# A graph-attention layer's softmax step and its feed-forward parts: one row copied by another engine, one more part a chunk in the last block

## The chip, the cores and the metric

The kernel runs on one core of a Trainium2 chip. The metric is the device time in microseconds (us) of one launch. The engines are TensorE (PE, matrix products; PEld is its weight load), VectorE (DVE), ScalarE (ACT), GpSimd (POOL, which issues the indirect gathers and scatters) and SyncE (SP, which issues the plain transfers). Each works off its own queue in order, and they meet through semaphores.

## The reference, cut to what matters

There are two graph layers in a row over 1250 nodes with 512 features and 40000 edges; only the first is touched.

```
h = layer_norm(x, ln1_g, ln1_b)                         # first layer
xl, xr = (h @ Wl), (h @ Wr)                             # 8 heads of 64
e  = einsum(leaky_relu(xl[src] + xr[dst], 0.2), att)    # a score per edge and head
m  = segment_max(e, dst);  ex = exp(e - m[dst])
h  = segment_sum(ex / denom[dst] * xl[src]) + gat_bias  # softmax over a node's edges
x1 = x + h
x1 = x1 + gelu(layer_norm(x1) @ W1 + b1) @ W2 + b2      # feed-forward, 512 -> 2048 -> 512
x  = layer_norm(x + x1)
...                                                     # second layer: relu(x[src] + edge features), sums, two dense layers
```

## The kernel before, in words

**Tiling.** The nodes are sorted by their number of edges and laid out in ten blocks of 128, one node a partition. `KB` (L699) gives the edge slots of each block: 44, 40, 37, 35, 33, 32, 31, 29, 27, 25. The blocks go in `ORDER` (L714) from block 9 down to block 0, so block 0, with the most edges, is the last one of the first layer. A block's slots are cut into groups (L1677 to L1680) of at most 20; block 0 has groups of 20, 16 and 8, block 1 of 16, 16 and 8, the others have two. There are 22 groups. A group is cut into chunks of at most `CN` = 5 slots; 77 chunks in all. The three groups of block 0 have 4, 4 and 2 chunks.

**A chunk.** `scores` (L1540) has POOL gather one row of `xl_t` per slot into a tile `xg` (seven buffers, `GB`), forms the score with four DVE instructions and writes it to the group's tile `S`, one row of eight heads per slot. After a group's last chunk `softmax` (L1559) finds the running maximum `m`, puts the older maximum into the row behind the group's scores, and subtracts; `exp` (L1572) makes the weights `w` of the scores and of that last row, which is the factor by which the sums so far must shrink. `weigh` (L1588), which runs one group behind the scores, multiplies the rows of `xg` by `w` (some rows on ACT, the rest on DVE) and adds them up on PE in `sums`; `leave` (L1615) folds the two sums into `pacc`, and `merge` (L1627) adds that to the block's `acc`. A buffer of `xg` is free for the next gather when PE has added it up.

**A finished block.** `head_of` (L1388) makes the residual sum, the layer norm and its transpose `hT`. `body_of` (L1441) is the feed-forward: 16 slices of 128 hidden features, in steps that the code calls parts. A part is four products into `pu`, a Gelu on ACT from `pu` to `uT` (one part later), and a product of `uT` (three parts later) into `py`. There is one `py` buffer, so only one block's feed-forward runs at a time. `end_of` (L1467) makes the last norm `xo`, adds the bias to give `order` (a reused tile) and scatters it into `xb_t`. The second layer, `second` (L1774), gathers from `xb_t` and can begin only when all ten blocks are there.

**The order of the work.** Every engine's queue is written out by the Python loops: `inorder` (L775) ties each instruction of DVE, ACT, PE and POOL behind the one recorded before. The main loop (L1686 to L1739) goes over groups and chunks. In each chunk it records the scores, steps the blocks that are between attention and end (`step_others`, L1504; in block 0 once more ahead of the scores, L1703), and spends a `quota` (L1726) of feed-forward parts with `some` (L1528), which calls `part` (L1519); `part` does nothing where no block is ready. The quota is 4 where a block waits for its feed-forward (`ready`), else 3. After the last group, what is left is recorded without a quota (L1740 to L1752).

Of the kernel before, what the change touches and what calls it, by code (L numbers as in the profile page):

```python
# [11 lines left out]
OP = mybir.AluOpType  # L12
AX = mybir.AxisListType
# [700 lines left out]
ORDER = range(NB - 1, -1, -1)  # L714
# [11 lines left out]
def gnn_kernel(ctx, tc, x, src, dst, edge_attr, ln1_g, ln1_b, Wl, Wr, att, gat_bias,  # L726
# [48 lines left out]
    def inorder(engine):  # L775

        latest = {}

        class Kept:
            def __getattr__(self, name):  # L780
                def call(*args, **kw):
                    ins = getattr(engine, name)(*args, **kw)  # L782
                    if latest:
                        tc.add_manual_dep(ins.ins, latest["ins"].ins.name, no_sync, reason="order of the program")
                    latest["ins"] = ins
                    return ins
                return call
        return Kept()
# [25 lines left out]
    with ExitStack() as s0:  # L814
# [18 lines left out]
        V, A, T = (inorder(e) for e in (nc.vector, nc.scalar, nc.tensor))  # L833
# [412 lines left out]
    def attention(s1, xb_t, xo_t, eb_t, back, lone, follow):  # L1246
# [8 lines left out]
        V, A, T, G = (inorder(e) for e in (nc.vector, nc.scalar, nc.tensor, nc.gpsimd))  # L1255
# [34 lines left out]
        def normed_of(b):  # L1290
            blk = dict(b=b, xn=bp.tile([P, D], F32, name="xn"))
            get(blk["xn"], hn_t, v_c[:, b:b + 1])
            return blk

        def slots_of(b):

            s_n = ap.tile([P, KB[0]], I32, name="s_n")
            s_f = ap.tile([P, KB[0]], F32, name="s_f")
            get(s_n[:, 0:KB[b]], src_v, w_i[:, b:b + 1])
            for _ in range(3):  # L1300
                yield
            to_src(V, s_f[:, 0:KB[b]], s_n[:, 0:KB[b]], b)
# [8 lines left out]
        def rows_of(blk):  # L1311
            held["xx"] += 1
            blk["xx"] = bp.tile([P, D], F32, name="xx", bufs=3)
            get(blk["xx"], x, v_c[:, blk["b"]:blk["b"] + 1])
# [31 lines left out]
        def wr_order():  # L1346

            w_t = w1[:, 0, :].rearrange("p (k d) -> p k d", k=KD)
            yield "late"
            pts = []  # L1350
            for k in range(KD):
                pts.append(aq.tile([P, KD, P], F32, name="pt1", tag="pu", bufs=4))
                for r in range(KD):
                    T.transpose(pts[k][:, r, :], wr[:, r, k * P:(k + 1) * P], ident)
            yield
            for k in range(KD):
                A.copy(w_t[:, k, :], pts[k].rearrange("p r n -> p (r n)"))
            yield "late"
            pms = []
            for r in range(KD):  # L1360
                pms.append(aq.tile([P, KD, P], F32, name="pm", tag="pu", bufs=4))
                for k in range(KD):
                    T.matmul(pms[r][:, k, :], w_t[:, k, r * P:(r + 1) * P], order[:, k, :], start=True, stop=True)
            yield
            for r in range(KD):
                A.copy(wr[:, r, :], pms[r].rearrange("p k n -> p (k n)"))

        done, ready, going, others, pres, lates = [], [], [], [], [], []
# [128 lines left out]
        def step_pres():  # L1497

            todo = list(pres)
            pres.clear()  # L1500
            for t in todo:
                step(t)

        def step_others():  # L1504

            if done and not held["head"]:
                held["head"] = 1
                others.append(head_of(done.pop(0)))
            for t in list(others):
                step(t)  # L1510
# [15 lines left out]
        quota = [0]  # L1526

        def some(n):  # L1528
            for _ in range(min(n, quota[0])):
                quota[0] -= 1  # L1530
                part()

        def drain(what, most):
            while held[what] > most:
                step_pres()
                step_others()
                part()
                step_lates()

        def scores(g, c):  # L1540

            c0, cn = g["cuts"][c]
            xg = gp.tile([P, CN, XW], F32, name="xg")
            for j in range(cn):
                at = KO[g["b"]] + g["k0"] + c0 + j
                get(xg[:, j, :], xl_t, src_i[:, at:at + 1])
            z = ap.tile([P, CN, XW], F32, name="z")
            z4, x4 = (t.rearrange("p n (h c) -> p n h c", c=CX)[:, :cn] for t in (z, xg))
            nxr = g["blk"]["nxr"]
            for op, c_, d_ in ((OP.max, 0, RIGHT + 1), (OP.min, RIGHT + 1, CX)):  # L1550
                V.tensor_tensor(z4[:, :, :, c_:d_], x4[:, :, :, c_:d_],
                                nxr[:, None, :, c_:d_].to_broadcast([P, cn, HEADS, d_ - c_]), op=op)
            zm = z4[:, :, :, LEFT + 1:RIGHT + 1]
            V.tensor_tensor(zm, zm, sgn[:, None, :, :].to_broadcast([P, cn, HEADS, MID]), op=OP.mult)
            V.tensor_reduce(g["S"][:, c0:c0 + cn, :].rearrange("p n h -> p (n h)"),
                            z[:, :cn, :].rearrange("p n (h c) -> p (n h) c", c=CX), axis=AX.X, op=OP.add)
            g["xg"].append(xg)

        def softmax(g):  # L1559

            n, S, blk = g["n"], g["S"], g["blk"]
            m_old = blk["m"]
            m = sp.tile([P, HEADS], F32, name="m")
            V.tensor_reduce(m, S[:, :n, :].rearrange("p n h -> p h n"), axis=AX.X, op=OP.max)
            V.tensor_tensor(m, m, m_old, op=OP.max)
            V.tensor_copy(S[:, n, :], m_old)
            blk["m"] = m
            g["w"] = w = sp.tile([P, GN + 1, HEADS], F32, name="w")
            V.tensor_tensor(S[:, :n + 1, :], S[:, :n + 1, :], m[:, None, :].to_broadcast([P, n + 1, HEADS]),
                            op=OP.subtract)  # L1570
# [112 lines left out]
        blk = dict(b=ORDER[0], nxr=nxr9)  # L1683
        ahead = weighing = None
        piece = [0]
        for i, g in enumerate(groups):  # L1686
            if g["first"]:
                if i:
                    blk, ahead = ahead, None
                blk["m"] = low  # L1690
                if g["b"] == 0:
                    drain("acc", 2)
                    held["acc"] += 1
                    blk.update(over)
                    blk["acc"] = bp.tile([P, D], F32, name="acc", bufs=3)
                    nc.sync.dma_start(blk["acc"], oa_t)
            g["blk"] = blk
            g["S"] = sp.tile([P, GN + 1, HEADS], F32, name="S", bufs=2)
            nc_ = len(g["cuts"])
            left = len(groups[i - 1]["cuts"]) if i else 0  # L1700
            for c in range(nc_):
                step_pres()
                if g["b"] == ORDER[-1]:  # L1703
                    step_others()
                scores(g, c)
                if c == nc_ - 1:
                    softmax(g)
                if c == 0:
                    if not i:
                        others.append(wr_order())  # L1710
                    if g["first"] and g["b"] != ORDER[-1]:
                        others.append(slots_of(g["b"] - 1))
                    if g is groups[-1] and held["xx"] < 3:
                        rows_of(blk)
                    weighing = weigh(groups[i - 1]) if i else None
                if folded:
                    merge(folded.pop())
                if c == 1 and g["first"] and g["b"] != ORDER[-1]:
                    ahead = normed_of(g["b"] - 1)
                if c == 2 and g["first"] and ahead:  # L1720
                    others.append(xr_of(ahead))
                if i > 3 and piece[0] < len(pieces):
                    piece_of(piece[0])
                    piece[0] += 1
                step_others()
                quota[0] = 4 if ready else 3  # L1726
                todo = -(-left // (nc_ - c))
                left -= todo
                for _ in range(todo):
                    next(weighing)  # L1730
                if left == 0 and weighing:
                    next(weighing, 0)
                if not todo:
                    for _ in leave():
                        some(1)
                if c == nc_ - 1:
                    exp(g)
                some(quota[0])
                step_lates()  # L1739
# [281 lines left out]
```

## Time and profile before

| | us |
|---|---|
| median of three runs | 1482.53 (1481.47 to 1487.09) |
| the profiled execution's own time | 1477.38 |
| its span, first to last instruction | 1475.5 |
| first gather of the attention | 85.7 |
| block 0's first softmax / last scores end | 772.8 / 830.7 |
| last block's attention ends (acc) | 851.7 |
| last scatter into `xb_t` / first gather from it | 899.6 / 903.6 |
| last gather of the second layer | 1329.5 |

Busy shares of the span: PE 79%, DVE 78%, POOL 59%, ACT 48%. The mean granted TensorE clock is 0.917 of full speed. In a profile line of the timeline, the first number is the start in us, the second the duration in us, then the engine, the source line (L782 stands for all calls through the recording helper), the operation, out<-in by tile names with partitions and elements, how many instructions are merged (PE counts each fp32 product as two), and in brackets the idle time before it and what ended it. A line of waits has the waiting instruction, the one it waited for, the total in us, the number of waits and the longest. A line of windows has the length, each engine's busy us with its instructions, the granted clock (PEclk), the share of the DMA queues and GB/s. In the page's strips a digit is the busy share of a fortieth of the span, in tenths.

### The profile page before, as it was taken

The page shows a single profiled execution, that of the slowest core. Times are in us where ns is not written, and L with a number is a line of the kernel's source. Part 1 is how long each engine was busy: PE and PEld are TensorE (multiplying, and loading weights), DVE is VectorE, ACT ScalarE, POOL GpSimd, SP SyncE. Part 2 cuts the span into 40 slices and gives each one's busy share as a digit, 9 for nine tenths or more (in the row PEclk, how much of TensorE's full clock was granted, in tenths as well). Part 3 has the DMA queues.
Part 4 walks back from the last instruction along what each step waited for, and adds up shares of the span by engine and source line. Part 5 has one row for each costly group of instructions (what it writes and reads, how often), then busy time and mean ns, then how long its engine had stood idle before and what let it go on. Part 6 is the DMA issues. An engine that isn't in the chain of part 4 may idle for free. (4 is left out here: it accounts for less than half of the span.)

```text
span 1475.5 us, 16467 instructions
## 1 busy us (share of the span) xinstructions
PE 1168.7 (79%) x5204; PEld 557.0 (38%) x5204; DVE 1146.9 (78%) x1472; ACT 710.4 (48%) x2033; POOL 864.8 (59%) x789
## 2 busy tenths in 40 slices
PE   6845659898988886969787896778786998988893
PEld 4431114344544442424244363222222443335452
DVE  7859898978888889797799713988888789877133
ACT  4526366867777675776858641111111222221533
POOL 2367877755677777774754004777777777750002
PEclk9977779999999798989898998999999999999996
DMA  6246966655566756653644144778777788750001
GB/s 235 90 139 184 393 189 175 181 147 152 153 192 176 207 167 191 173 155 110 172 121 112 32 156 145 243 237 247 242 242 231 233 246 249 235 161 22 0 0 72
DMA packets 89151, 251.16 MB, mean 170 GB/s; under 512 B 17214, under 2 KB 19268, under 8 KB 88543
## 3 DMA queue, kind: packets, MB, share of 16 engines
q0 software_dynamic: 61008, 199.11, 46.5%
q1 hardware_dynamic: 28047, 50.91, 9.7%
q8 instruction: 43, 0.70, 0.2%
q14 instruction: 53, 0.43, 0.1%
HBM read 225.86 MB, written 24.22 MB: 169 GB/s over the span
## 5 line engine op out<-in xcount | busy, mean ns | idle before, releaser
L782 POOL DMA_INDIRECT xg<-xl_t,src_i x333 | 421.2, 1265 | 192.6 <-issue 113.5
L749 POOL DMA_INDIRECT xs<-xb_t,src_i x333 | 314.8, 945 | 115.0 <-issue 67.9
L782 ACT ACTIVATE xg<-xg,w 128x64 f32<-128x64 f32 x1296 | 323.2, 344 | 0.1
L782 PE MATMUL sums<-xg,ident 64*64 64x512 f32 x1332 | 208.1, 699 | 110.0 <-DVE xg L782 103.2
L1829 PE MATMUL pe<-we,eaT 64*128 64x512 f32 x666 | 201.5, 663 | 72.4 <-DVE xs L1874 67.9
L782 DVE TENSOR_TENSOR z<-xg,nxr 128x1440 f32<-128x1440 f32 (+4 forms) x154 | 197.7, 1324 | 41.0 <-DMA xg<-xl_t,src_i 40.0
L782 DVE TENSOR_REDUCE S<-z 128x32 f32<-128x2080 f32 (+2 forms) x77 | 192.2, 2496 | 2.6
L782 PEld LDWEIGHTS pu<-hT,w 128*128 128x128 f32 x1280 | 165.1, 198 | 67.5 <-issue 57.6
L1874 DVE TENSOR_TENSOR xs<-xs,pe 128x1024 f32<-128x1024 f32 (+1 forms) x130 | 153.3, 1186 | 36.8 <-DMA xs<-xb_t,src_i 24.5
L782 PE MATMUL py<-w,uT 128*128 128x512 f32 x320 | 164.7, 606 | 15.5 <-ACT uT L782 15.4
L782 PE MATMUL pu<-hT,w 128*128 128x128 f32 x1280 | 173.6, 284 | 0.0
L1875 DVE SCALAR_TENSOR_TENSOR pd<-xs,pd 128x1024 f32<-128x1024 f32 (+1 forms) x130 | 155.7, 1197 | 3.3
L782 PEld LDWEIGHTS sums<-xg,ident 64*64 64x64 f32 x1332 | 58.1, 152 | 249.8 <-DVE xg L782 127.6
L1829 PEld LDWEIGHTS pe<-we,eaT 64*128 64x128 f32 x666 | 58.3, 192 | 169.5 <-DVE xs L1874 119.1
L1871 ACT ACTIVATE xs<-pe 128x1024 f32<-128x1024 f32 x40 | 41.0, 1024 | 163.9 <-PE pe L1870 126.3
L782 DVE TENSOR_TENSOR xg<-xg,w 128x1024 f32<-128x1024 f32 (+2 forms) x77 | 102.2, 1332 | 0.0
L782 ACT ACT_TABLE_LOAD x73 | 93.7, 1283 | 7.9 <-DVE sh L782 4.3
L1870 PE MATMUL pe<-xs,ident 128*128 128x512 f32 x160 | 88.3, 662 | 3.9 <-DMA xs<-xb_t,src_i 3.7
L741 POOL DMA_INDIRECT out_dram<-z,v_i x10 | 10.0, 1003 | 130.9 <-ACT z L782 128.4
L782 PE MATMUL pacc<-ab,fold 128*64 128x512 f32 x88 | 54.3, 703 | 40.1 <-ACT ab L782 38.8
L782 DVE TENSOR_TENSOR z<-z,sgn 128x768 f32<-128x768 f32 (+2 forms) x77 | 78.2, 1016 | 0.0
L782 PE MATMUL pz<-z,v 128*128 128x512 f32 (+1 forms) x192 | 71.1, 530 | 6.0 <-ACT z L782 6.0
(264 smaller groups left out, 1286.5 us busy)
## 6 DMA issues: line engine op xcount, KB each, us to landing
eb_t<-fe SPq DMA_DIRECT2D x38, 256.0 KB
ea<-eb_t SPq DMA_DIRECT2D x38, 256.0 KB
w<-in_L_gnn_W_dram SPq DMA_DIRECT2D x8, 1024.0 KB
xg<-xl_t,src_i POOLq DMA_INDIRECT x333, 3.9
xs<-xb_t,src_i POOLq DMA_INDIRECT x333, 3.8
v<-in_L_gnn_W_dram SPq DMA_DIRECT2D x2, 2048.0 KB
xo_t<-xo SPq DMA_DIRECT2D x10, 256.0 KB
x_out<-xo_t SPq DMA_DIRECT2D x10, 256.0 KB
```

What stands on the lines that cost most here:

```text
L741: s = nc.gpsimd.indirect_dma_start(out=table, out_offset=bass.IndirectOffsetOnAxis(ap=idx, axis=0), in_=rows, in_offset=None, bounds_check ...
L749: return nc.gpsimd.indirect_dma_start(out=rows, out_offset=None, in_=table, in_offset=bass.IndirectOffsetOnAxis(ap=idx, axis=0))
L782: ins = getattr(engine, name)(*args, **kw)
L1829: nc.tensor.matmul(pe[:, k, :], eaTs[n][r, j // 2, :], we[r, :], start=True, stop=not by_pe(i))
L1870: nc.tensor.matmul(pe[:, k, :], ident, xs[:, k, :], start=False, stop=True)
L1871: nc.scalar.activation(xv, pe, AF.Relu)
L1874: add = nc.vector.tensor_add(xv, xv, pe[:, :m, :])
L1875: nc.vector.scalar_tensor_tensor(pv, xv, 0.0, pv, op0=OP.max, op1=OP.add)
```

## The change

The softmax no longer forms the new maximum in two steps. ACT copies the older maximum into the row behind the group's scores when the group's tile is made, ahead of its first chunk; the reduction then takes that row along, and a combining step and a copy on DVE are left out. Separately, the quota is 4 in all chunks of block 0, not only in those in which a block is ready.

```diff
         def softmax(g):
 
             n, S, blk = g["n"], g["S"], g["blk"]
-            m_old = blk["m"]
             m = sp.tile([P, HEADS], F32, name="m")
-            V.tensor_reduce(m, S[:, :n, :].rearrange("p n h -> p h n"), axis=AX.X, op=OP.max)
-            V.tensor_tensor(m, m, m_old, op=OP.max)
-            V.tensor_copy(S[:, n, :], m_old)
+            V.tensor_reduce(m, S[:, :n + 1, :].rearrange("p n h -> p h n"), axis=AX.X, op=OP.max)
             blk["m"] = m
...
             g["blk"] = blk
             g["S"] = sp.tile([P, GN + 1, HEADS], F32, name="S", bufs=2)
+            A.copy(g["S"][:, g["n"], :], blk["m"])
             nc_ = len(g["cuts"])
...
                 step_others()
-                quota[0] = 4 if ready else 3
+                quota[0] = 4 if ready or g["b"] == ORDER[-1] else 3
                 todo = -(-left // (nc_ - c))
```

In the queues that come out, DVE has 44 instructions fewer and ACT 22 copies more. In block 0 six of the feed-forward parts of block 1 stand ahead of the last group's `w` that stood behind it before, ACT loads its function tables four times fewer, the end of block 2 (`xo`, `order` and, on POOL, its scatter into `xb_t`, ten instructions earlier) comes two chunks sooner, and one small load of `ea` on SP changes places with its neighbour. The other instructions stand in the order they had.

## The prediction

> **What bounds the kernel now.** I read the page's slices, then the waits, then the timeline by engine around the two edits. VectorE (DVE) is at 8 or 9 tenths through the first layer, TensorE (PE) close behind, so a DVE saving can count there and a PE addition can hurt.
>
> ```profile
> PE   6845659898988886969787896778786998988893
> DVE  7859898978888889797799713988888789877133
> DVE z L782 <- DMA xg<-xl_t,src_i: 40.0, 16, 5.9
> POOL xb_t L782 <- DVE order L782: 83.6, 3, 53.2
> ```
>
> The third line (waits) says that DVE is not the bound throughout: in 16 places it waits for gathered rows. The fourth is the turn to the second layer: GpSimd (POOL) cannot gather from xb_t before block 0, the last, is through its feed-forward.
>
> A group's softmax, from DVE's timeline:
>
> ```profile
> 808.40 0.38 DVE L782 TENSOR_REDUCE m<-S 128x8 f32<-128x128 f32 x1
> 808.82 0.17 DVE L782 TENSOR_TENSOR m<-m 128x8 f32<-128x8 f32 x1
> 808.90 0.17 DVE L782 COPY S<-m 128x8 f32<-128x8 f32 x1
> 809.10 0.30 DVE L782 TENSOR_TENSOR S<-S,m 128x136 f32<-128x136 f32 x1
> ```
>
> And block 0's end:
>
> ```profile
> 815.38 0.69 DVE L782 TENSOR_TENSOR order<-xo,be_b 128x512 f32<-128x512 f32 x1 [4.58 <-ACT xo L782]
> 833.84 0.26 ACT L782 ACTIVATE w<-S 128x72 f32<-128x72 f32 x1
> 836.52 0.26 DVE L782 TENSOR_REDUCE gd<-w 128x8 f32<-128x64 f32 x1
> 850.99 0.69 DVE L782 TENSOR_TENSOR acc<-acc,t 128x512 f32<-128x512 f32 x1
> 865.32 0.69 DVE L782 TENSOR_TENSOR xx<-xx,py 128x512 f32<-128x512 f32 x1 [7.54 <-PE py L782]
> 866.05 1.12 PE L782 MATMUL py<-b,one 1*128 1x512 f32 x2 [0.78 <-DVE xx L782]
> 869.64 0.37 ACT L782 ACTIVATE uT<-pu,cols 128x128 f32<-128x128 f32 x1
> ```
>
> The last group's weights (w) come 2.7 us before DVE wants them (836.52). Attention ends at 851.68; block 0's feed-forward starts only at 866.05, when block 1's has left py; its first Gelu is at 869.64.
>
> **Edit 1: the softmax.** Of 0.70 us from m<-S to S<-S,m (808.40 to 809.10), 0.42 is the reduction's own step (to 808.82). Eight more elements add 0.01 (383 ns for 128 inputs, 396 for 136). So a group saves 0.70 - 0.43, about 0.26; 22 groups, 5.8 us of DVE. ScalarE (ACT) pays 22 copies; nearest row, COPY oden<-pd 128x8 at 172 ns: 3.8 us, on an engine 48% busy. [...]
>
> The reduction now waits for ACT. The order of the changed kernel has the copy right behind the previous group's w<-S, which ran at most about 5 us after its scores (809.10 to 814.33), while the next reduction comes 18 us later or more (709.49 to 727.56). So it costs nothing; if ACT were later, the reduction, this group's exp and the next multiply would stand behind it, and with them the buffers that POOL waits for.
>
> How much of 0.26 a group arrives, by DVE's waits. Groups 1 to 3 end before it waits for rows at 159.09: lost. Groups 4 to 9 (188.6 to 358.9) see no such wait: 6 x 0.26 = 1.6. Groups 10 to 13 (398 to 509) lie where POOL issues almost back to back (383 to 531) and DVE waits for rows six times: lost. Groups 14 to 17: half, 0.5. Groups 18 and 19: 0.5. Sum 2.6 (bounds 0 and 5.0 for the 19 groups). Against it the ACT copies where ACT is the late one: bounds 0 and 19 x 0.17 = 3.2; I take 0.5, as most of ACT's time has gaps. Up to block 0: -2.1.
>
> **Edit 2: four parts a chunk in block 0.** No work is added; the order decides. Of block 1's 16 Gelus, 9 stood before the last group's w<-S and 7 behind; now 15 and 1. ACT has four table loads fewer. [...] here a load starts at 868.35 and the Gelu behind it at 869.64, so 1.29, 5.2 in all. [...]
>
> *The tail gains.* From acc (851.68) to block 0's hT nothing stands between any more: transposes 0.97 with their wait, aT 1.14, px 1.10, sum 0.72, statistics 0.94, root 0.33, two small ones 0.5, h 0.85, transposes 0.7, hT 1.51: 8.8 us. Then xo of block 1, one table load and the first Gelu, about 11.5 after acc. Before it was 18.0 (851.68 to 869.64). Gain 6.5.
>
> *The block loses.* (a) Block 2's body ends sooner, so its xo and order<-xo move from the start of the last group to two chunks before. There DVE stands in front of order<-xo; ACT's xo stands behind hT of block 1, that behind PE's transposes of h, those behind the sums of the chunk that DVE has just multiplied (about 795.3). Sums 2.79, transposes 0.66, hT 1.5, xo 0.8: DVE waits 5.8 instead of 4.58. Moreover PE has had nothing since the sums of the chunk before (about 787), 8 us, and after a shorter rest it ran at half clock:
>
> ```profile
> 801.27 5.38 PE L782 MATMUL sums<-xg,ident 64*64 64x512 f32 x20 [3.81 <-DVE xg L782]
> core 0: us, PE busy (x) PEld busy (x) DVE busy (x) ACT busy (x) POOL busy (x), PEclk, DMA share, GB/s
> 801.00:807.00 6.00, 5.73 (x21) 1.98 (x22) 5.90 (x8) 5.97 (x22) 3.61 (x3) 0.52 0.57 164
> ```
>
> The same sums took 2.79 at clock 1.00. So another 0 to 2.6; I take 2.3. (b) From there on PE is the chain, since a part holds it 1.75 us (Gelus at 874.54, 876.30). Without the half clock: order at 801.1, order 0.7, scores of four rows 5.5, multiply 1.75: the third chunk's sums start at 809.1 and take 2.7; four parts 7.0; sums 2.7; four parts 7.0; 828.5. The two pacc steps 2.75 (820.50 to 822.25, and 1.0), two chunks' sums 3.7: 835.0. Three parts to the last Gelu that w<-S stands behind, 2 x 1.75 + 1.05 + 0.3 = 4.9; eight row products 1.9, table load 1.3, w 0.3: 843.4. DVE wanted w at 836.5: late by 6.9, and by 9.2 with the half clock. The rest of the attention follows it step by step.
>
> Sum of edit 2, with block 0's three softmaxes in it: +9.2 - 6.5 = +2.7; bounds +0.4 (full clock) and, if the cover were ample, -6.5.
>
> POOL: the scatter to xb_t of block 2 moves ahead of ten instructions, so four gathers and an xx gather and four more stand behind it. It waits for order, about 804; the first four rows then land by about 813 and are wanted at 818, the last four (free once the third chunk's sums are done, 814) at 827. Free. SP swaps one small ea load: free.
>
> **Total.** -2.1 + 2.7 = +0.6. The profiled execution took 1477.38 (span 1475.5), so 1478.0 for its like. It lies 5 us under the median 1482.53, below all three timed runs; the sum is a difference, so I put it on the median: 1483.1, say 1483.
>
> **Rivals.**
> 1. *The extra parts fit under DVE.* DVE has one wait in 750 to 838, and PE is busy 74 of those 88 us, 14 free for 10.5 us of six parts. Against: the sums and the Gelus stand in one order, so gaps before sums are not free for parts behind them. Then the tail's 6.5 stays, and -2.1 and 0.8 for three softmaxes: -9.4, 1473. Chance 0.12.
> 2. *PE stays cold (slower).* Place: block 0 from 795 to 843. With more waits inside it, PE falls to half clock again and again; the chain of eleven parts and four sums, about 34 us, stretches. Before, 800 to 838 was granted 0.91. It decides from about 0.75: 34 x (0.91/0.75 - 1) = 7.3 us more, +8, 1491. Chance 0.14.
> 3. *Edit 1 arrives whole,* the block at full clock: -5.0 + 0.4, 1478. Chance 0.16.
> 4. *Edit 1 is lost to waits for rows and to ACT:* 0.5 + 2.7, 1486. Chance 0.16.
>
> **Numbers.** The likeliest, 1483, has 0.42, with about 3 us either side. About 0.5% (7.4 us) is what a measurement can tell from no change. Faster by more: rival 1's, 0.12. Slower by more: rival 2's and an edge of rival 4, 0.15. Within: 0.73. The range goes from 1476 to 1489: it holds the likeliest, 3 and 4, and leaves most of 1 and 2 out.
>
> **What would show it.** Step 1: S<-S,m 0.44 us behind m<-S, no wait for ACT in m<-S. Step 2: order<-xo waits 6 to 8 us two chunks earlier; a wait of 6 us or more of gd for w in the last group; attention's last acc 6 to 9 us later, counted from block 0's start; the first Gelu of block 0 about 11.5 us behind acc instead of 18. Wrong if gd doesn't wait (rival 1), if the clock in that stretch is under 0.8 (rival 2), or if m<-S waits for ACT.

## The result, and the profile after

The changed kernel takes 1486.92 us (median of 15 runs, 1482.27 to 1491.26), the kernel before, timed beside it, 1482.28 (15 runs, 1477.43 to 1487.09): ratio 1.004, 95% interval 1.003 to 1.0051, so 4.4 to 7.6 us slower. The forecast was 1483, within 0.5% of before. The measured difference reaches to the edge of that 0.5%, on the slow side.

The profiled execution of after took 1488.24 us (span 1486.5), 11.0 us more than that of before. Cut at four events, the two spans differ like this:

| stretch | before | after | difference |
|---|---|---|---|
| start to block 0's acc<-px,xx | 784.41 | 784.89 | +0.48 |
| "the block": from there to the end of the last acc<-acc,t | 67.27 | 80.16 | +12.89 |
| "the tail": from there to the second layer's first gather | 51.89 | 45.73 | -6.16 |
| second layer to the end | 571.9 | 575.7 | +3.8 |

The last line is no effect of the change: the four kernels e1 to e4 below, with one part of the change or both, have 572.4 to 572.9 there. What is left, +7.2, goes with the measured 4.4 to 7.6.

DVE's timeline of after, the softmax of a group of block 0, its end and the last group. The columns are start, duration, engine, line, operation, tiles and shapes, and in brackets the idle time before it with the releaser:

```profile
804.03 0.69 DVE L782 TENSOR_TENSOR order<-xo,be_b 128x512 f32<-128x512 f32 x1 [8.24 <-ACT xo L782]
...
817.48 0.40 DVE L782 TENSOR_REDUCE m<-S 128x8 f32<-128x136 f32 x1
817.91 0.30 DVE L782 TENSOR_TENSOR S<-S,m 128x136 f32<-128x136 f32 x1
...
849.80 0.27 DVE L782 TENSOR_REDUCE gd<-w 128x8 f32<-128x64 f32 x1 [8.10 <-ACT w L782]
...
864.36 0.69 DVE L782 TENSOR_TENSOR acc<-acc,t 128x512 f32<-128x512 f32 x1
```

The softmax is two steps, 0.43 us apart, and m<-S waits for nobody (in all 22 groups together 0.5 us). The sum order<-xo stands two chunks earlier and waits 8.24 us. The last group's gd waits 8.10 us for w; before it waited not at all.

PE's timeline of after in the same stretch:

```profile
795.85 5.32 PE L782 MATMUL sums<-xg,ident 64*64 64x512 f32 x20 [7.98 <-DVE xg L782]
...
802.74 3.84 PE L782 MATMUL pu<-hT,w 128*128 128x128 f32 x32
809.55 1.12 PE L782 MATMUL py<-w,uT 128*128 128x512 f32 x2 [2.97 <-ACT uT L782]
811.97 5.38 PE L782 MATMUL sums<-xg,ident 64*64 64x512 f32 x20 [1.30 <-DVE xg L782]
817.29 1.50 PE L782 MATMUL pu<-hT,w 128*128 128x128 f32 x8
...
824.84 2.79 PE L782 MATMUL sums<-xg,ident 64*64 64x512 f32 x20
...
836.57 1.07 PE L782 MATMUL pacc<-ab,fold 128*64 128x512 f32 x2 [0.73 <-ACT ab L782]
...
848.37 1.95 PE L782 MATMUL sums<-xg,ident 64*64 64x512 f32 x16
```

The same 20 sums take 2.79 us at full clock (at 824.84, granted 1.00), and twice here 5.3 to 5.4, at about half of it (granted 0.52 and 0.50): once behind a rest of 7.98 us and once behind two short rests of 2.97 and 1.30. From 811.97 to 850.32 PE has one gap, of 0.73 us. So in the stretch that ends with the last w it is PE that sets the time.

The view of windows, for the block alone, before and then after (columns: length, then busy time of PE, PE's weight loads, DVE, ACT and POOL, the granted clock, DMA share, GB/s):

```profile
784.41:851.68 67.27, 54.46 (x312) 23.87 (x310) 54.41 (x68) 48.38 (x148) 17.62 (x14) 0.95 0.26 75
```

```profile
784.89:865.05 80.16, 63.24 (x350) 29.63 (x350) 53.91 (x64) 47.94 (x153) 19.55 (x14) 0.89 0.21 62
```

PE is busy 8.8 us longer (a net 38 matmul records more, for the parts drawn forward, and one more stretch at half clock) and idle 4.1 us longer (16.9 instead of 12.8): together the 12.9. DVE and ACT do the same work as before.

### The profile page after: what moved, and what is told of

The parts are those of the page before. It is cut to its first block, busy times and chain, and to the rows that moved or that the text cites. A ratio compares the mean times of both kernels' runs of the same rounds, so it can differ in the third digit from the quotient of the medians.

```text
span 1486.5 us, 16450 instructions
## 1 busy us (share of the span) xinstructions
PE 1174.3 (79%) x5204; PEld 559.2 (38%) x5204; DVE 1141.4 (77%) x1428; ACT 708.3 (48%) x2051; POOL 873.8 (59%) x789
## 5 line engine op out<-in xcount | busy, mean ns | idle before, releaser
L782 POOL DMA_INDIRECT xg<-xl_t,src_i x333 | 429.7, 1290 | 185.3 <-issue 102.3
L1827 PE MATMUL pe<-we,eaT 64*128 64x512 f32 x666 | 204.8, 674 | 72.6 <-DVE xs L1872 68.0
L782 ACT ACTIVATE uT<-pu,cols 128x128 f32<-128x128 f32 x160 | 55.5, 365 | 46.8 <-PE pu L782 46.0
```

Of the source, the lines that this page charges most:

```text
L1827: nc.tensor.matmul(pe[:, k, :], eaTs[n][r, j // 2, :], we[r, :], start=True, stop=not by_pe(i))
```

## The experiments

Theory 1: the time is lost where DVE stands in front of order<-xo. Theory 2: PE's chain loses it; the six parts now stand in front of the last sums on PE, whatever DVE does. Rival: the softmax loses it (22 ACT copies, or rows that come late).

The first four runs were timed on a chip on which the kernel before takes 1481 us, as above; the later ones on two others, on which it takes 1598 and 1609 us. Ratios are always to the kernel before on the same chip. From the profiles of the other chips only the block and the tail are compared, in which equal instructions last equally long (20 sums at full clock 2.79 us, z<-xg,nxr of five slots 2.93 to 2.94 on all three). Each row has one profile. How much that can differ show e1 and f3, whose instructions in the block are the same: 67.74 and 70.37. So differences of up to some 2.6 us in one block are not told from chance.

| run | ratio, 95% interval | block | tail | both |
|---|---|---|---|---|
| before | 1 | 67.27 | 51.89 | 119.16 |
| after | 1.004, 1.003 to 1.0051 | 80.16 | 45.73 | 125.89 |
| e1 softmax only | 1.0011, 0.9993 to 1.0028 | 67.74 | 51.90 | 119.64 |
| e2 parts only | 1.0041, 1.0028 to 1.0054 | 79.82 | 45.71 | 125.53 |
| e3 order later | 1.002, 1.0007 to 1.0033 | 76.97 | 47.31 | 124.28 |
| e4 last exp first | 1.0042, 1.0024 to 1.0059 | 80.15 | 45.73 | 125.88 |
| f1 order and scatter later | 1.0037, 1.0018 to 1.0056 | 77.03 | 47.20 | 124.23 |
| f2 extra matmuls | 1.0102, 1.0052 to 1.0152 | 82.30 | 45.71 | 128.01 |
| f3 weights later | 1.0066, 1.0041 to 1.0091 | 70.37 | 51.88 | 122.25 |
| f4 softmax, order later | 1.0012, 0.9992 to 1.0031 | 67.80 | 51.88 | 119.68 |
| g1 matmuls in the gap | 1.0059, 1.0038 to 1.008 | 79.79 | 45.69 | 125.48 |
| g3 early transposes | 0.999, 0.9964 to 1.0017 | 68.64 | 48.83 | 117.47 |
| g4 the same, order later | 1.0013, 0.9984 to 1.0041 | 68.56 | 48.85 | 117.41 |
| g5 early transposes, quota 3 | 0.9958, 0.9936 to 0.998 | 67.17 | 49.49 | 116.66 |

### Which part costs: e1 and e2

e1 is the kernel before with the softmax and the ACT copy alone; e2 is it with one line alone:

```diff
-                quota[0] = 4 if ready else 3
+                quota[0] = 4 if ready or g["b"] == ORDER[-1] else 3
```

> The kernel before with the softmax part of the change alone (ACT's copy of the older maximum behind the scores, one reduction over n+1 rows); quota stays 3. My theory (the softmax helps a little, the four parts cost the time): ratio to before 0.997 to 1.000, about 1480, with S<-S,m 0.38 to 0.49 us behind m<-S in every group and attention up to block 0 shorter by 1 to 3 us. Rival A (the 22 ACT copies, or a DVE that arrives earlier at the gathers, cost what the changed kernel lost): 1.003, about 1487, and the waits of DVE for rows grow. Rival B (all of the 5.5 us that DVE is less busy arrives): 0.996, about 1477.

> The kernel before with the quota of four parts a chunk in block 0 alone; the softmax stays as it was. My theory (this is what costs): ratio 1.003 to 1.005, about 1487 to 1489; order<-xo waits 7 to 9 us near 804, gd of the last group waits 6 us or more for w, attention ends 12 to 13 us later, the tail is 6 to 7 us shorter. Rival A (the softmax costs): 1.000 within 0.001.

The four parts alone cost 1.0041, as much as the whole change, with the block and the tail of after. The softmax alone cannot be told from nothing: its medians are 1484.58 and 1481.49. I had expected attention up to block 0 to be 1 to 3 us shorter; in its profile block 0 starts 0.7 us earlier (783.70 instead of 784.41). It shows two places where the gain goes. DVE's timeline of e1:

```profile
146.50 1.22 DVE L782 TENSOR_TENSOR xg<-xg,w 128x1024 f32<-128x1024 f32 x1
152.45 2.94 DVE L782 TENSOR_TENSOR z<-xg,nxr 128x1800 f32<-128x1800 f32 x2 [4.73 <-DMA xg<-xl_t,src_i]
...
807.76 0.30 DVE L782 TENSOR_TENSOR S<-S,m 128x136 f32<-128x136 f32 x1
815.41 0.69 DVE L782 TENSOR_TENSOR order<-xo,be_b 128x512 f32<-128x512 f32 x1 [5.95 <-ACT xo L782]
```

In group 3 DVE waits 4.73 us for rows. And S<-S,m of block 0's second group is 1.34 us earlier than before (809.10), but order<-xo, which waited 4.58, now waits 5.95 and starts at 815.41 (before 815.38): all of it given back.

### Where the wait at order<-xo goes: e3, e4, f1, f4

e3 is the changed kernel with the sum behind the yields, for block 2 alone:

```diff
-            V.tensor_add(xb, xo, be_b)
+            if b != 2:
+                V.tensor_add(xb, xo, be_b)
             for _ in range(4 if b else 0):
                 yield
+            if b == 2:
+                V.tensor_add(xb, xo, be_b)
```

> The changed kernel, but block 2's DVE sum order<-xo stands one chunk later on DVE's queue, behind the next chunk's scores and multiply; nothing else is moved. Theory 1 (the wait of DVE for xo is what costs; behind it the third chunk's multiply, its sums and with them the chain of parts up to the last w are late): DVE's wait of 8.2 us goes, the sums that ran at half clock at 811.97 start 8 us earlier and take 2.7 instead of 5.4; gd gets w about 10 us earlier; the whole 1476 to 1478, ratio 0.996 to 0.997. Theory 2 (PE's chain of eleven parts with its half clock sets w by itself, wherever DVE stands): the wait only moves to gd, which then waits 13 us or more; the whole within 3 us of the changed kernel's 1487, ratio 1.001 to 1.003.

The sum moved two chunks. DVE's timeline of e3:

```profile
805.63 0.68 DVE L782 TENSOR_TENSOR order<-xo,be_b 128x512 f32<-128x512 f32 x1
815.72 2.39 DVE L782 TENSOR_TENSOR z<-xg,nxr 128x1440 f32<-128x1440 f32 x2 [9.40 <-DMA xg<-xl_t,src_i]
...
841.92 0.27 DVE L782 TENSOR_REDUCE gd<-w 128x8 f32<-128x64 f32 x1 [5.77 <-ACT w L782]
```

and POOL's, same run:

```profile
806.60 1.01 POOL L782 DMA_INDIRECT xb_t<-order,v_i  x1 [17.18 <-DVE order L782]
807.92 0.97 POOL L782 DMA_INDIRECT xg<-xl_t,src_i  x1 [0.30 <-ACT xg L782]
```

The 8.24 us in front of the sum became 9.40 in front of rows: the scatter of order stands on POOL's queue ahead of the next four gathers, and it waited with them. So the run does not tell the theories apart; f1 moves the scatter behind the gathers too (four more yields behind the sum).

> The changed kernel, but block 2's order<-xo stands two chunks later on DVE's queue and its scatter to xb_t stands behind all gathers of block 0 on POOL's. In the run that moved the order alone, the scatter held the gathers on POOL and DVE waited 9.4 us for rows instead of 8.2 us for xo, so it told little. Theory 2 (PE's chain: from block 0's second chunk on PE is busy nearly without a gap, and the six parts that were drawn forward, 10.5 us, are in front of the last w whatever DVE does): neither wait is left, but gd now waits 10 us or more for w; from block 0's start (acc<-px,xx) to the last acc 73 to 77 us, against 67.3 before and 80.2 in the changed kernel; ratio 1.000 to 1.002. Theory 1 (DVE's waits set it): gd waits less than 4 us, 66 to 70 us, ratio 0.995 to 0.997.

DVE's timeline of f1:

```profile
828.21 0.68 DVE L782 TENSOR_TENSOR order<-xo,be_b 128x512 f32<-128x512 f32 x1
839.17 0.38 DVE L782 TENSOR_REDUCE gd<-w 128x8 f32<-128x128 f32 x1 [4.53 <-ACT w L782]
...
864.55 0.27 DVE L782 TENSOR_REDUCE gd<-w 128x8 f32<-128x64 f32 x1 [8.11 <-ACT w L782]
```

Now DVE waits neither for xo nor for rows, and the block still takes 77.03: the wait stands at w, in two places, 12.6 us. Theory 1 is out: of the 12.9 us DVE's stand is worth at most 3.1, of which 1.8 are PE's shorter busy time (61.40 instead of 63.24, at a granted clock of 0.93 instead of 0.89). (The ratio, 1.0037, is above what I had set for theory 2, 1.000 to 1.002; the block is at the top of its 73 to 77.)

e4 takes the last chunk's four parts and most of its row products from in front of the last w on ACT:

```diff
                 if c == nc_ - 1:
                     softmax(g)
+                    if g is groups[-1]:
+                        exp(g)
...
-                if c == nc_ - 1:
+                if c == nc_ - 1 and g is not groups[-1]:
                     exp(g)
```

> The changed kernel, but in the last group's last chunk ACT's w<-S is issued right behind the softmax, ahead of that chunk's four parts and most of its row products (two table loads more). Theory 2 (parts in front of the last w cost the time): w 7 to 9 us earlier, gd waits less than 2 us, attention ends 5 to 8 us earlier, the tail gains 0 to 3 less since the four parts come behind; the whole 1480 to 1483, ratio 0.999 to 1.000. Theory 1 (the time was lost at order<-xo, the wait at gd only passes it on): less than 3 us are won, 1485 or more, ratio 1.002 or more.

DVE's timeline of e4:

```profile
840.19 0.26 DVE L782 TENSOR_REDUCE gd<-w 128x8 f32<-128x64 f32 x1
842.32 0.68 DVE L782 TENSOR_TENSOR acc<-acc,w 128x512 f32<-128x512 f32 x1
854.21 0.69 DVE L782 TENSOR_TENSOR acc<-acc,pacc 128x512 f32<-128x512 f32 x1 [11.21 <-PE pacc L782]
```

w was there in time, and nothing was won: the wait went to pacc, whose matmul stands behind the same four parts on PE. The block is 80.15, after's 80.16. My expectation of 1480 to 1483 was wrong; that the parts are ahead of w on ACT is not what costs. On PE they are still ahead of the last sums.

f4 is e1 with e3's edit. With quota 3 the scatter is behind the gathers anyway, and the sum now comes behind the block's last acc (868.52).

> The softmax part alone with quota 3 (no four parts), and block 2's order<-xo two chunks later on DVE's queue; its scatter stays where it is, behind all gathers. The softmax alone came to block 0's third softmax 1.3 us earlier and gave it all back at order<-xo, which waited 5.95 instead of 4.58 us. If DVE sets the end of block 0 there: that wait goes, the last acc 3 to 6 us earlier, whole 1477 to 1480, ratio 0.997 to 0.999. If PE sets it (busy nearly without a gap from 801 to 838): gd or acc<-acc,pacc waits longer by what was won, last acc within 2 us, ratio 0.9995 to 1.001.

DVE's timeline of f4:

```profile
833.38 0.38 DVE L782 TENSOR_REDUCE gd<-w 128x8 f32<-128x128 f32 x1 [1.29 <-ACT w L782]
853.34 0.27 DVE L782 TENSOR_REDUCE gd<-w 128x8 f32<-128x64 f32 x1 [5.05 <-ACT w L782]
```

e1's wait of 5.95 is now 1.29 and 5.05 in front of w, and the block 67.80 against 67.74. So PE sets block 0 with three parts a chunk as well, and an earlier DVE gained nothing. One reservation: f4's PE was busy 2.4 us longer than e1's (58.07 against 55.72), at a clock of 0.87 instead of 0.95. Up to that much an earlier DVE could have won, had the clock been e1's.

### The half clock: f2 and g1

Both put twelve extra matmuls into the changed kernel, whose result nobody reads:

```diff
+                if c == 1 and g is groups[-3]:
+                    warm = aq.tile([P, D], F32, name="warm", tag="pu", bufs=4)
+                    for _ in range(12):
+                        T.matmul(warm, ident, w2[:, 0, :], start=True, stop=True)
                 for j in range(cn):
```

> The changed kernel with twelve extra matmuls of 128x512 (their result is not read) in the 8 us in which PE waits for block 0's second multiply, so that its clock does not fall. If the half clock is part of the cost: the clock of the 6 us behind is 0.9 to 1.0 instead of 0.50, the sums take 2.8 instead of 5.2 us, the wait at order<-xo falls from 8.2 to 5.5 to 6, the last acc comes 2.3 to 2.6 us earlier, ratio 1.002 to 1.003. If the clock is of no account (the wait at gd takes up what is won): the last acc within 1 us, ratio 1.004.

f2 had groups[-4] there, one group too early: its matmuls ran before block 0 began, px came 3.90 us late, and the rest of PE in front of the second sums stayed (7.90 us, sums 5.13). It says nothing on the clock.

> The changed kernel with the twelve extra matmuls of 128x512 (result not read) now in the right place, one group later than in the run before: between the first and the second chunk's sums of block 0, where PE waits 8 us for DVE. Theory (the half clock is a part of the cost): the second chunk's sums take 2.8 instead of 5.2 us at a clock near 1.00; order<-xo waits 5.5 to 6 us; from acc<-px,xx to the last acc 77.5 us instead of 80.2. Rival (the wait at gd takes it up): the stretch stays within 0.7 us of 80.2.

PE's timeline of g1:

```profile
810.33 10.57 PE L782 MATMUL warm<-w,ident 128*128 128x512 f32 x24
820.83 2.79 PE L782 MATMUL sums<-xg,ident 64*64 64x512 f32 x20
...
834.42 5.38 PE L782 MATMUL sums<-xg,ident 64*64 64x512 f32 x20 [1.29 <-DVE xg L782]
```

With PE busy, the second sums take 2.79 instead of 5.32. But the twelve matmuls took 10.57 us, not the 8 I had room for: from acc<-px,xx the sums start 13.4 us in, after's 11.0. They lost in front what the clock won behind, and the block moved by 0.4 only. So the half clock's 2.5 us are shown at the sums, and what they are worth at the block's end is not. The third sums are at half clock again.

### The rows in group 3: f3

f3 is e1 with the feed-forward weights (8 transfers on SP) released 40 us later:

```diff
                 ins = A.copy(blk["acc"], pacc)
-                if g["b"] == ORDER[0]:
-                    load_ffn(ins)
...
-                A.copy(t, pa)
+                load_ffn(A.copy(t, pa))
```

> The softmax part alone, with the load of the feed-forward weights (8 transfers) released 40 us later, behind block 9's last copy instead of its first. In all four profiles with the new softmax DVE waits 4.3 to 4.7 us for a chunk of rows near 153, in the two with the old one it does not: the chunk's last gathers go out just behind the start of the weights instead of just ahead. If that is so: no such wait, group 3 about 4 us earlier than in the run of the softmax alone; what is won is given back at groups 10 to 14, where DVE waits for rows anyway, so the whole moves by 2 us at most: ratio 0.998 to 1.001. If POOL's own pace causes the wait: it stays at 4 us or more. If what happened at group 3 does carry to the end: ratio 0.997 or less.

Rows gathered between 135 and 144 us, landing times, in the view of the tile xg, of before and then of e1:

```profile
L782 POOL DMA_INDIRECT xg<-xl_t,src_i x6: 942/1104/1300, 136.6 to 143.5; - x6
...
DMA to landing us min/median/max: 3.7/3.8/5.7
```

```profile
L782 POOL DMA_INDIRECT xg<-xl_t,src_i x6: 946/1100/1302, 135.3 to 143.8; - x6
...
DMA to landing us min/median/max: 3.8/4.5/8.6
```

In both kernels SP starts the weights at 143.4 to 143.7. In e1 the chunk that DVE wants at 148 has its last row gathered at 143.75, behind that start, and it lands 8.6 us later. In before its last row went out at 142.27. From group 1's to group 3's S<-S,m the old softmax takes 44.4 to 45.2 us (3 profiles, on two chips), the new one 48.3 to 51.9 (10 profiles, three chips), f3 46.1. DVE's wait there is 4.73 in e1 and 1.29 in f3. So the burst, the eight transfers close together, is the cause of most of the wait. But f3 pays for it later, in DVE's timeline and in POOL's:

```profile
233.33 2.94 DVE L782 TENSOR_TENSOR z<-xg,nxr 128x1800 f32<-128x1800 f32 x2 [8.67 <-DMA xg<-xl_t,src_i]
```

```profile
222.27 0.95 POOL L782 DMA_INDIRECT fe<-in_edge_attr_dram,wx  x1 [17.16 <-DVE S L782]
```

It is slower than before, 1.0066, where I expected no more than 1.001. This second wait is another one. The last of its rows goes out at 229.54 and lands within 3.8 us; the rows are late because POOL stood 17.16 us in front of a gather of edge features (fe) that is ahead of them in its queue. The store that empties fe, eb_t<-fe, now stands behind the weights on SP, at 211.16. That POOL waited for it is likely but not shown, since the profile names DVE. Another 2.6 us of f3's loss lie in block 0, which has e1's instructions.

### Parts into the gap: g3, g4, g5

If PE's idle time is the cost, it must help to put parts into it. g3 is the changed kernel with block 1's transposes of h, and hT, ahead of the second sums:

```diff
-            yield from place()
+            if blk["b"] != 1:
+                yield from place()
+            else:
+                held["ps"] += 1
             pt = aq.tile([P, KD, P], F32, name="pt2", tag="pu", bufs=4)
...
             held["h"] = 0
-            yield
+            if blk["b"] != 1:
+                yield
```

g4 has f1's edit too; g5 has g3's edit on the kernel before (old softmax, quota 3).

> The changed kernel, but the transposes of block 1's h and its hT go out one place earlier, ahead of the second chunk's sums in block 0, so that four parts of block 1 stand in the 8 us in which PE waits for DVE (nothing else is changed; quota stays 4). Theory (PE's work is the same, what counts is its idle time before the last w): PE's idle time of 8 us and the two half-clock stretches go, gd's wait for the last w falls from 8.1 to under 3 us; from acc<-px,xx to the last acc 68 to 74 us instead of 80.2, the tail 44 to 46; both together 114 to 119 against 125.9 and, before, 119.2; ratio 0.997 to 1.000. Rival (ACT is then the late one: hT, Gelus, a table load and 24 row products ahead of the second sums): stretch 77 us or more, ratio 1.002 or more.

> As the run with the early transposes, and block 2's order<-xo two chunks later with its scatter behind block 0's gathers. If DVE's stand at order<-xo still costs with PE filled: a further 2 to 5 us, stretch 65 to 70, ratio 0.995 to 0.998. If PE is still the bound: within 1 us of the early transposes alone.

> The kernel before (old softmax, quota 3) with the early transposes alone. Theory: the stretch falls from 67.3 to 62 to 66 us if PE's idle time was the cost, with the tail at 50 to 53 (7 Gelus or so behind the last w): ratio 0.996 to 0.999; if DVE already bounds the kernel before there, the stretch stays at 66 to 68 and the ratio at 0.999 to 1.001. Compared with the early transposes at quota 4 it tells whether the fourth part pays once PE has room for it.

PE's timeline of g3:

```profile
811.58 0.66 PE L782 MATMUL pt<-ident,h 128*128 128x128 f32 x4 [0.99 <-ACT h L782]
812.16 1.12 PE L782 MATMUL py<-b,one 1*128 1x512 f32 x2
813.21 3.84 PE L782 MATMUL pu<-hT,w 128*128 128x128 f32 x32
819.51 1.12 PE L782 MATMUL py<-w,uT 128*128 128x512 f32 x2 [2.46 <-ACT uT L782]
820.57 2.79 PE L782 MATMUL sums<-xg,ident 64*64 64x512 f32 x20
...
830.55 2.79 PE L782 MATMUL sums<-xg,ident 64*64 64x512 f32 x20
```

and DVE's, same run:

```profile
822.61 0.69 DVE L782 TENSOR_TENSOR order<-xo,be_b 128x512 f32<-128x512 f32 x1 [4.10 <-ACT xo L782]
859.75 0.27 DVE L782 TENSOR_REDUCE gd<-w 128x8 f32<-128x64 f32 x1 [1.49 <-ACT w L782]
```

The block's windows, of g3 and of g5:

```profile
807.60:876.24 68.64, 59.48 (x354) 28.79 (x354) 53.86 (x65) 47.43 (x152) 18.57 (x14) 1.00 0.26 73
```

```profile
795.88:863.05 67.17, 57.29 (x342) 26.47 (x340) 54.61 (x68) 49.53 (x151) 17.12 (x14) 1.00 0.26 74
```

The same parts, put into the gap instead of behind it, make the block 68.64 instead of 80.16: PE's idle time goes from 16.9 to 9.2 us, the clock from 0.89 to 1.00. That is the plainest evidence for theory 2. The rival that I had set against it, ACT as the late engine (77 us or more), is out. The tail is 48.83, 3.1 us longer than after's and 2.8 above the 44 to 46 that I expected. PE now has no parts left to do between block 0's own first steps; px takes it 2.08 us instead of 1.05 (the granted clock of the whole tail is 0.83 instead of 0.93), and the first products into pu begin 10.7 us behind acc instead of 7.5. Both together are 1.7 shorter than before, which is within the scatter of one profile. g4 shows that DVE's remaining 4.10 us at order<-xo cost nothing that can be measured (68.56). g5 keeps the block at before's length (67.17; I had hoped for 62 to 66) with more of the parts done in it, and its tail is 2.4 us shorter.

g5 is the only kernel faster than before, 0.9958 (0.9936 to 0.998), some 3 to 10 us, and it contains neither part of the change. The 2.5 us of its block and tail are about as much as the near end of that interval, but within the scatter of one profile. Where the gain comes from stays open, since no profile of before was taken on that chip.

## Why the prediction was right, and where it was not

The whole came out inside the range and about within the 0.5%, but 4.6 us slower in the median where 0.6 was forecast. It is rival 4 that happened ("edit 1 is lost", 1486), with a size of edit 2 that was too small. Both terms erred to the slow side, by some 2 and 4 us; that their sum still lies inside a range of 6 us to that side is in part luck.

- **Edit 1, the saving.** Right: 0.43 us from m<-S to S<-S,m, no wait for ACT. Where DVE has no wait, a group is shorter by the 0.26 taken from the row: from S<-S,m to S<-S,m group 19 takes 18.65 to 18.67 us with the old softmax and 18.37 to 18.41 with the new, group 7 28.60 to 28.63 and mostly 28.29 to 28.31.
- **Edit 1, what arrives: "up to block 0: -2.1". This step failed.** Groups 1 to 3 were put at nothing ("lost"), and they were a loss. From group 1's to group 3's softmax the four profiles with the new softmax on the first chip take 48.3 to 48.8 us, before 44.4, because of the rows behind the weights. From group 3's to group 19's they take 568.3 to 568.5, before 571.6: 3.1 to 3.4 us won, more than forecast, and used up by the first three groups. (The second stretch is good to some 4 us only in a single profile: e2, with the old softmax, has 576.0.) In block 0 the rest went into the wait at order<-xo. For the whole time e1's interval, -1.0 to +4.1 us, leaves -2.1 out.
- **Edit 2, order<-xo.** Right: 8.24 us two chunks earlier against 5.8 + 2.3, and the first sums at half clock (granted 0.52), 5.32.
- **Edit 2, "late by 9.2". The mechanism was right, the term too small.** w should have come at 843.4 + 2.3 = 845.7; it was done at 849.8, 3.6 us late if block 0's later start of 0.5 is taken off. Of this 2.6 is the third sums at half clock (5.38 instead of 2.79), which the chain had at full clock; the remaining 1.0 stays open. The prediction was right that "from there on PE is the chain", but I did not see that PE would rest 2.97 us for uT and 1.30 for DVE there. Counted through to the last acc it is 12.9 in after and 12.6 in e2.
- **Edit 2, the tail.** Right: 6.16 gained against 6.5; the first Gelu of block 0 comes 10.8 us behind acc. The prediction said 11.5, but the terms it lists add up to 10.9. At this Gelu 7.1 us are won; 1.0 is lost again before the gather, where the first 32 products into pu take 5.47 us at a granted clock of 0.69 instead of 3.84 at 1.00. The table load there starts at 874.57 and its Gelu at 875.87, 1.30 apart, against the 1.29 that the prediction read from the row of before, so that reading held.
- **POOL's scatter "free".** So in the change itself: DVE waits for no rows in block 0. e3 shows the cover: with the order two chunks later the same scatter costs 9.4.
- **Sum.** Edit 2: 12.9 - 6.2 = +6.7 in the profile, +6.4 in e2's, whose ratio gives 4.1 to 8.0; forecast +2.7. Edit 1: no gain, -1.0 to +4.1 by e1.
- **Rivals.** 1 is out (gd waits). 2 ("PE falls to half clock again and again") came half true: a second time, at 813 to 819 with a granted clock of 0.58, but 0.87 over its stretch from 795 to 843, above the 0.75 from which it was to decide. 3 is out.

## What to carry to other kernels

Before drawing work forward on an engine, count that engine's idle time between the new place and the point that sets the end, and see whether the work goes into the gap or behind it: behind it the six parts cost 12.9 us to win 6.2, in it the block came out at 68.6 instead of 80.2. That cost is not only the added work: the sums behind the open gap of 7.98 us took 5.32 us in after, at a granted clock of 0.52, and 2.79 in g1 and g3, where the gap had work in it. A wait that is moved is not removed: the 8 us at order<-xo turned up at w or at pacc, wherever DVE was placed, because PE was the late one (and in e3 at rows, behind the scatter). And a step that is made shorter ahead of a burst of transfers can put the next gathers behind the burst (in e1 one landed after 8.6 us, and DVE waited 4.73); what such a step wins arrives only where nothing else is waited for.

## What the runs showed of the hardware

- When PE falls to half clock does not follow from the length of one rest. Behind two rests of 2.97 and 1.30 us with 1.12 us of work between, 20 sums took 5.38 us in after (granted clock 0.50), and behind 2.98 and 1.29 with 1.13 between just as long in g1. Behind a rest of 3.46 and 1.12 us of work in g5, 16 sums took 1.95 us, as 16 do at full clock in before; the granted clock of g5's whole block was 1.00. The same place in before and then in e1, with almost the same rests:

```profile
791.38 1.12 PE L782 MATMUL py<-w,uT 128*128 128x512 f32 x2 [0.90 <-ACT uT L782]
794.08 2.79 PE L782 MATMUL sums<-xg,ident 64*64 64x512 f32 x20 [1.57 <-DVE xg L782]
```

```profile
790.68 1.12 PE L782 MATMUL py<-w,uT 128*128 128x512 f32 x2 [0.88 <-ACT uT L782]
793.00 4.49 PE L782 MATMUL sums<-xg,ident 64*64 64x512 f32 x20 [1.20 <-DVE xg L782]
```

The granted clock during these sums was 1.00 and 0.61. What decides between the two is not shown here.
- In e1, with eight weight transfers started on SP, the gather just behind their start landed after 8.6 us, where six gathers had a median of 3.8 in before. In after the longest of the same six took 8.6 as well.
- The kernel before takes 1482, 1598 or 1609 us on three chips. The large DVE sums of the second layer last equally long in before, f4 and g5 (1.22 us), but from 930 to 1300 us DVE waits in front of them 22.5 us on the first chip and 92.8 and 79.7 on the others. From the second layer's first gather to the end it is 572 to 576 us on the first and 677 to 687 on the others. Why stays open.
